# A Gram matrix from the high halves in 512-column matmuls, and image columns in the value product, in a two-layer cross-attention kernel

## The chip, the cores and the metric

The kernel runs on one core of a Trainium2 chip. The metric is the time of one execution on the device in microseconds (us), as a median of runs. The engines are TensorE (PE, matmuls; PEld is its weight load), VectorE (DVE), ScalarE (ACT), GpSimd (POOL), and SyncE (SP), which here issues nearly all of the DMA transfers, in the order of its queue.

## What is computed

Two cross-attention layers run one behind the other on the same text context, in fp32. Both have 16 batches of 256 queries, 20 heads of 16 columns, and a context of 256 tokens of 512 features. Layer 1 takes 77 of these as text and 179 as image tokens. In layer 2, which the change concerns, the last four are image tokens and the other 252 text. Layer 2, cut:

```python
probs_t = softmax(q @ k_t.T * scale)             # per head, over 252 text tokens
text_out = probs_t @ v_t
qsem = probs_t @ text_ehs                        # per head: 256 x 512
qsem = qsem / max(norm(qsem), EPS)               # _l2norm
ip_n = ip_ehs / max(norm(ip_ehs), EPS)
sem = qsem @ ip_n.T                              # per head: 256 x 4
probs_ip = softmax(q @ k_ip.T * scale + 0.5 * sem) * spatial_mask
out = (text_out + probs_ip @ v_ip) @ W_out + b_out + hidden_states
```

The kernel never forms qsem. With p a row of probs_t and E the text tokens, its product with an image token is p (E e_ip), four more columns beside the values, and its squared norm is the quadratic form p (E E^T) p^T. E E^T, 252 x 252 for each batch, is the Gram matrix.

## The kernel before

An fp32 operand is held as two halves, a rounded high one and a low one (the remainder), each in a form that PE reads fast. A product (`prod`, L325) is the sum high x high, high x low, low x high, over the tiles of 128 of the contraction: 12 matmuls for 512 features.

Layer 2 runs in 80 slots of one head group (4 heads) each, five slots to a batch (`slot1`); the slots of the layer before overlap with its beginning. In each slot, for two halves t of 128 rows, PE computes scores T of the slot (L1018) and scores S of a later slot with rows and columns exchanged (L1023), of which DVE takes the maxima (`mn`, L1024) and a copy of the image columns (`sr`, L1040). There is one bank pair for S, so the second S comes when both have been read. ACT takes the exponentials (L1030); PE multiplies them with the values (L1088, L1090). For the norm, PE multiplies the Gram blocks (`gm`, seven of 128 x 128: four high, three low) with the rounded exponentials `ctb`, seven matmuls of 512 columns for each t (L1075, in `norm1`); DVE multiplies and adds the results (L1078, L1080), with POOL's part (L1080) and POOL's low halves (L1066) beside it.

Around the slots run tasks of a batch, each a generator that yields between its steps: `keys1` (k1: three row blocks m of the keys, L651 or L325 on PE, the image columns on POOL, L652, the low half on DVE, L655, then out to memory, kd, and back in slot form, ks), `tokens1` (t1: values, Gram), the opening `o1` (queries: high and low halves `hq`, L706 to L709, product L725, out as qd and back as qs), the image softmax `i1` (u, L1159 and L1161) and the close `c1` (three row products of the image part, L1209 on PE, L1210 on DVE, the halves `ho` by ACT, L981, and DVE, L972 and L974, then the output product L725 and L996).

The table `STEPS` (L45) gives each step a slot time relative to its batch's first slot, in five fill positions (.2 apart) of each slot; a step is recorded when its time comes, so the order in which PE, DVE, ACT and POOL work in layer 2 is that of the program. `late` puts off a DVE evacuation to a fixed place behind the slot's own work. SP's queue is ordered by the scheduler.

`tokens1` has five steps: values of rows 0 to 127, values of rows 124 to 251 (DUP = 124; a mask `tmask` keeps double rows from counting twice), Gram of these two row blocks, and a last one that scales a block. A Gram step is one `prod`: the tokens are both operands, 12 matmuls of 256 columns. Columns 252 to 255 of the Gram product are E e_ip, which DVE multiplies with 1 / norm (`rn`) into the value tile (L679, L693); ACT rounds the others to `gm` (L675, L676, L683, L684) and DVE takes the low halves (L678, L687, L690).

## Time and profile before

| | |
|---|---|
| median of 3 runs | 1455.69 us (1451.59 to 1458.66) |
| profiled execution, span | 1449.8 us |
| PE busy in the span | 1401.7 us, 97% |
| DVE busy | 1174.2 us, 81% |
| POOL busy | 1152.3 us, 79% |
| ACT busy | 937.6 us, 65% |
| one batch of layer 2, steady | 48.15 us (five slots) |

The span is the profiled execution's own time; the runs have a few microseconds around it, 5.9 for the median. A row of a timeline gives the start, the time from the first start to the last end of the row's instructions, the engine, the line, the operation, out<-in by the program's names, partitions x elements, and the count; in brackets the idle time before, and what ended it. Matmuls overlap in the records, so what a run of them takes is read from start to start.

### The profile page before, as it was taken

How to read it: one execution, taken by the hardware profiler on the slowest of the kernel's cores; microseconds unless marked ns; L12 is line 12 of the kernel's file. 1: busy time of each engine (PE TensorE's matmuls, PEld its weight loads, DVE VectorE, ACT ScalarE, POOL GpSimd, SP SyncE). 2: the span in 40 equal slices, each digit the busy share in tenths (PEclk: the TensorE clock that was granted, in tenths of full speed). 3: DMA queues.
4: the chain of work that ended last, by engine and by line, in shares of the span. 5: the costliest groups of instructions: out<-in, count | busy, mean ns of one | idle time of the engine just before them, and what ended most of it. 6: DMA issues, size and time to landing. Idle time of an engine off the chain costs nothing.

```text
span 1449.8 us, 35042 instructions
## 1 busy us (share of the span) xinstructions
PE 1401.7 (97%) x12166; PEld 1157.8 (80%) x12166; DVE 1174.2 (81%) x2570; ACT 937.6 (65%) x2075; POOL 1152.3 (79%) x1181
## 2 busy tenths in 40 slices
PE   7899999999999999889999999999999999999998
PEld 6788888888888888577777788878878888888865
DVE  5477777777777788867888888988998889888887
ACT  5567676767676776755666666666666666566553
POOL 4269797979787878887778887788778877887785
PEclk9999999999999999999999999999999999999999
DMA  6866575665656578575544444544454445444411
GB/s 200 197 161 181 143 186 147 163 169 155 168 151 171 145 201 232 133 188 155 158 123 124 143 141 125 154 137 140 130 150 138 139 135 149 139 136 131 130 33 50
DMA packets 236284, 215.74 MB, mean 149 GB/s; under 512 B 57834, under 2 KB 222732, under 8 KB 236108
## 3 DMA queue, kind: packets, MB, share of 16 engines
q1 hardware_dynamic: 233886, 212.53, 53.4%
q8 instruction: 97, 1.59, 0.5%
q10 hardware_dynamic: 2222, 0.98, 0.3%
q14 instruction: 79, 0.65, 0.2%
HBM read 127.32 MB, written 85.16 MB: 147 GB/s over the span
## 4 chain that ended last, share of the span: by engine, by line
PE 52%; DVE 3%; POOL 1%; issue 1%; ACT 0%; DMA 0%; ACTq 0%; DVEq 0%; POOLq 0%
PE X L1075 18%; PE X L325 9%; PE X L725 6%; PE P L1088 5%; PE T L1018 4%; PE S L1023 3%; PE P L1090 2%; PE X L1209 1%; PE X L651 1%; PE P L1055 1%; DVE mn L1024 1%; PE P L934 1%; POOL P L902 0%; DVE wt L1078 0%; POOL wt L1066 0%
## 5 line engine op out<-in xcount | busy, mean ns | idle before, releaser
L902 POOL TENSOR_TENSOR P<-P,rs 128x512 f32<-128x512 f32 x320 | 412.4, 1313 | 136.1 <-ACT P L899 136.0
L1075 PE MATMUL X<-ctb,gm 128*128 128x512 f32 x1120 | 293.3, 403 | 0.7 <-DVE wt L1078 0.7
L1066 POOL TENSOR_TENSOR wt<-P,ctb 128x512 f32<-128x512 f32 x212 | 268.1, 1293 | 0.0
L899 ACT ACTIVATE P<-T 128x512 f32<-128x512 f32 x320 | 174.7, 594 | 101.8 <-PE T L896 83.7
L1024 DVE TENSOR_REDUCE mn<-S 128x4 fp32r<-128x1008 f32 x160 | 192.1, 1200 | 58.7 <-PE S L1023 56.8
L1075 PEld LDWEIGHTS X<-ctb,gm 128*128 128x128 f32 x1120 | 202.5, 190 | 38.5 <-DVE wt L1078 0.9
L1078 DVE TENSOR_TENSOR wt<-X,wt 128x512 f32<-128x512 f32 x240 | 159.7, 682 | 4.2 <-PE X L1075 3.9
L1030 ACT ACTIVATE P<-T 128x512 f32<-128x512 f32 x212 | 115.2, 598 | 58.3 <-PE T L1018 56.6
L1080 POOL TENSOR_TENSOR wt<-wt 128x512 f32<-128x512 f32 x80 | 103.5, 1294 | 60.2 <-DVE wt L1078 60.0
L876 DVE TENSOR_REDUCE mn<-S 128x4 fp32r<-128x716 f32 x160 | 142.5, 890 | 0.0
L1065 ACT ACTIVATE ctb<-P 128x512 fp32r<-128x512 f32 x212 | 122.4, 625 | 29.4 <-PE X L1075 20.6
L934 PE MATMUL P<-P,vr 128*32 128x256 f32 x1920 | 123.7, 388 | 0.0
L725 PE MATMUL X<-ho,wF 128*128 128x256 f32 x768 | 109.0, 286 | 2.2 <-DVE ho L974 1.2
L725 PEld LDWEIGHTS X<-ho,wF 128*128 128x128 f32 x768 | 100.5, 189 | 8.8 <-DVE ho L974 2.7
L725 PE MATMUL X<-hq,wE 128*128 128x256 f32 x720 | 102.7, 286 | 4.6 <-ACT hq L706 3.3
L725 PEld LDWEIGHTS X<-hq,wE 128*128 128x128 f32 x720 | 96.4, 193 | 8.3 <-ACT hq L706 3.8
L875 DVE TENSOR_REDUCE mn<-S 128x4 fp32r<-128x308 f32 x160 | 74.8, 468 | 23.2 <-PE S L874 22.9
L945 DVE STREAM_TRANSPOSE nt<-P 128x512 f32<-128x512 f32 x80 | 57.1, 714 | 39.2 <-PE P L934 38.9
L934 PEld LDWEIGHTS P<-P,vr 128*32 128x32 f32 x1920 | 56.1, 110 | 40.8 <-issue 4.9
L874 PE MATMUL S<-ks,qs 125*128 125x256 f32 x480 | 85.7, 301 | 2.2 <-DMA ks<-kd 1.7
L874 PEld LDWEIGHTS S<-ks,qs 125*128 125x128 f32 x480 | 64.4, 189 | 28.2 <-issue 24.1
L325 PE MATMUL X<-cta,wA 128*128 128x252 f32 (+3 forms) x534 | 78.8, 292 | 7.9 <-ACT wA L244 5.7
(231 smaller groups left out, 3275.3 us busy)
## 6 DMA issues: line engine op xcount, KB each, us to landing
qd<-q SPq DMA_DIRECT2D x80, 256.0 KB
qs<-qd SPq DMA_DIRECT2D x160, 112.0 KB
ks<-kd SPq DMA_DIRECT2D x160, 112.0 KB
rawc<-in_cT_dram SPq DMA_DIRECT2D x60, 256.0 KB
kd<-kst SPq DMA_DIRECT2D x50, 256.0 KB
qs<-qd SPq DMA_DIRECT2D x60, 192.0 KB
ks<-kd SPq DMA_DIRECT2D x60, 192.0 KB
qd<-q SPq DMA_DIRECT2D x64, 128.0 KB
```

What stands on the lines that cost most here:

```text
L325: last = mm(out, lhs(a, k), rhs(b, k), start=i == 0, stop=i == len(terms) - 1)
L725: mm(pp, w(s, k, slice(m * 128, (m + 1) * 128)), a[:, t], start=i == 0, stop=i == len(terms) - 1)
L874: mm(sp[:, h], Q[: XROW + T0, h, t * 128 : (t + 1) * 128], K[: XROW + T0, h], start=True, stop=True)
L876: anchor(nc.vector.tensor_reduce(mn[:, 1, :, t], sp[:, :, T0:], axis=AX.X, op=ALU.max))
L899: exp = anchor(nc.scalar.activation(pt, st[p], AF.Exp, scale=SCALE))
L902: anchor(nc.gpsimd.tensor_mul(pt, pt, rs[:, t : t + 1].to_broadcast([128, 2, S])))
L934: mm(pv[32 * s : 32 * s + 32, o : o + S], v[:, vt, h : h + 32], P[k, s // 2][:, t, s % 2], start=vt < 2, stop=vt != 1,)
L1024: anchor(nc.vector.tensor_reduce(maxes[k + 2][:, :, t], sp[:, :, :T1], axis=AX.X, op=ALU.max))
L1065: nc.scalar.activation(R[k, u][:, t], P[k, u][:, t], AF.Copy, scale=0.5)
L1066: anchor(nc.gpsimd.tensor_sub(W[k, u][:, t], P[k, u][:, t], f(R[k, u][:, t])))
L1075: mm(yp, gm[:, gb], R[k, u][:, kt], start=i == 0, stop=i == len(blocks[n]) - 1)
L1078: nc.vector.tensor_mul(product, yp, w[:, n])
```

## The change

**Gram.** A Gram step becomes four matmuls of 512 columns, one for each 128 features: the tokens' high half stands, and high and low halves of all 256 tokens move. The bank then holds g = high x high and x = high x low. The third term, low x high, is the transpose of x summed over both row blocks, and since the quadratic form is symmetric, the cross product may be doubled instead: the low blocks become g - rounded(g) + 2x. Where only one of two symmetric blocks is kept, the transposed cross block is needed: ACT copies it from the first Gram's bank (`turn`), and one 128-column matmul adds it, turned, in the second Gram's sum, behind its third 512-column matmul. DVE has two operations for each low block instead of one.

**Image columns.** They came from the Gram product with all three terms and now come from the value product, which grows from 320 to 324 columns. The value weights get four more columns at each side, into which POOL copies the batch's image tokens at step m = 1 of the keys (two copies). ACT copies the four columns out (`ip`), and DVE multiplies them with `rn` from there.

**Steps.** Times in the table move; in effect, in a steady batch: the third key block and its transfers, both value steps, both Gram steps, the last three steps of the opening, and steps of the image softmax and of the close. Line numbers grow by 2 to 26.

```diff
--- before.py
+++ after.py
@@ -54,18 +54,18 @@
     "s0o": (-2.4, -1.4, -1, -0.8, -0.4, 0.4, 1.6,),
     "c0e": (5.6, 6, 6.6, 7.2, 7.6, 8.2,),
     "c0o": (5.6, 6, 6.6, 7.2, 8.2, 9.2,),
-    "k1": (-7, -6.2, -6.2, -5, -4.2, -3.4,),
-    "t1": (-3.2, -2.2, -2.2, -1.4, -0.2,),
-    "o1": (-7, -6.8, -6, -5.8, -5.4, -3.4,),
-    "i1": (6.8, 7.6, 7.6, 8.8, 9.4, 9.6, 10.6, 10.8, 10.8, 12.2,),
-    "c1": (12.8, 12.8, 13.4, 14, 14, 15.8,),
-    ("i1", B - 2): (6.6, 7, 7.2, 7.2, 7.8, 8, 8.6, 9.2, 9.2, 9.6,),
+    "k1": (-7, -6.2, -6.2, -5, -4, -2.6,),
+    "t1": (-3.2, -2, -1.2, -1.2, -0.2,),
+    "o1": (-7, -6.8, -6, -4, -3.6, -0.6,),
+    "i1": (6.8, 8.2, 8.6, 8.6, 9, 9.6, 10.8, 10.8, 10.8, 12.2,),
+    "c1": (12.8, 12.8, 13, 13.6, 13.8, 17,),
+    ("i1", B - 2): (6.6, 7, 7.2, 7.2, 7.8, 8, 8.6, 8.8, 9.2, 9.6,),
     ("c1", B - 2): (9.8, 11.8, 11.8, 12.2, 12.4, 12.4,),
-    ("i1", B - 1): (6.8, 7.6, 7.8, 10, 10, 10, 11, 11, 11.2, 12,),
+    ("i1", B - 1): (6.8, 7.6, 7.8, 10, 10, 10, 11.2, 11.2, 11.2, 12,),
     ("c1", B - 1): (11.8, 11.8, 11.8, 11.8, 13.4, 16,),
-    ("k1", 0): (-7, -6.2, -5.8, -5, -4.6, -3,),
+    ("k1", 0): (-7, -6.2, -5.8, -5, -4.6, -3.4,),
     ("k1", 1): (-8, -6.2, -5.2, -5, -4.6, -3,),
-    ("t1", 0): (-3.6, -2.6, -2, -1.4, -0.4,),
+    ("t1", 0): (-3.6, -2.6, -1.2, -0.6, 0.4,),
     ("t1", 1): (-3, -2.2, -2.2, -1.2, -0.8,),
     ("o1", 0): (-7, -7, -5.6, -5.2, -4.4, -4.4,),
     ("o1", 1): (-6.8, -6.8, -6.2, -5.8, -4, -3.8,),
@@ -152,7 +152,7 @@
 
 
     clock = [-99.0]
-    words, slots = {"ctb": 1024, "cta": 1024, "raw": 512, "rawc": 512, "kb": 576, "mt": S, "mx": 2, "kst": 4 * S, "rs": 2 * S, "P": 4 * S}, {}
+    words, slots = {"ctb": 1024, "cta": 1024, "raw": 512, "rawc": 512, "kb": 576, "mt": S, "mx": 2, "kst": 4 * S, "rs": 2 * S, "P": 4 * S, "wC": 8 * (320 + 2 * NIP)}, {}
 
     def buf(tag, shape, dtype=F32, bufs=1, name=None):
         if tag in ("wB", "wD", "vr", "raw"):
@@ -217,6 +217,8 @@
     nc.scalar.copy(ident_r, ident)
     tmask = const_tile([128, 7], "tmask")
     dma(tmask, tmask_d)
+    tm2 = const_tile([128, 1], "tm2")
+    nc.vector.tensor_scalar_mul(tm2, tmask[:, 2:3], 2.0)
 
     anchors = {}
 
@@ -338,7 +340,13 @@
         yield from in_turn(parts, wait, *(("rawc raw", nc.vector) if b == 2 and n == 2 else ("rawc", nc.gpsimd)))
         if n == 2:
             return lambda s, k: tiles[k][:, s].rearrange("p (b t) -> p b t", b=2)
-        return lambda s, k: tiles[k // 2][:, s, (k % 2) * S : (k % 2 + 1) * S]
+
+        def view(s, k):
+            if isinstance(k, slice):
+                return tiles[k.start // 2][:, s].rearrange("p s (k t) -> p s k t", t=S)
+            return tiles[k // 2][:, s, (k % 2) * S : (k % 2 + 1) * S]
+
+        return view
 
 
     ct = [buf(t, [128, 2, 512], FR, bufs=2, name="ct") for t in ("cta", "cta", "ctb", "ctb")]
@@ -571,7 +579,9 @@
 
     def weights6():
         cip = w1["cip"]
-        _, text, w1["v"] = by_row(wv1_d, "wC")
+        wv = buf("wC", [128, 2, 4, 320 + 2 * NIP], FR)
+        text = [(wv1_d[k * 128 : (k + 1) * 128], wv[:, 0, k, NIP:-NIP], wv[:, 1, k, NIP:-NIP]) for k in range(4)]
+        w1["v"], w1["ip"] = lambda s, k, i: wv[:, s, k, NIP * i : NIP * i + 320 + NIP], lambda i: wv[..., (0, 320 + NIP)[i] :][..., :NIP]
         image, wvi1 = by_column(wvi1_d)
         yield from in_turn(text + image, 0.3, "rawc")
         vip = buf("rawc", [128, 512], bufs=2, name="vip")[:BI, :CP]
@@ -655,42 +665,58 @@
                 lambda kst=kst, kp=kp: nc.vector.tensor_sub(kst[:, 1, 0, :T1], kp, f(kst[:, 0, 0, :T1])),
                 lambda kst=kst, m=m: keys_out1(kd[1][b], m, kst[:, :, 0]),
             )
+            if m == 1:
+                for k in range(2):
+                    last = ct(slice(None), slice(2 * k, 2 * k + 2))[..., T1:]
+                    nc.gpsimd.tensor_copy(w1["ip"](b % 2)[:, :, 2 * k : 2 * k + 2], f(last))
             yield
 
     def tokens1(b):
         ct = ct1[b]
         V, G = v1t[b % 2], gmt[b % 2]
         vc = vcols(V, V1W)
-        for t, lo, sc in ((0, 0, 1.0), (1, DUP, tmask[:, 2:3])):
-            vp = bank()[:, :320]
-            prod(vp, lambda s, k: ct(s, k)[:, lo : lo + 128], w1["v"], 4)
-            nc.scalar.activation(vc[:, t, :, 0:16], vp.rearrange("p (h d) -> p h d", d=D), AF.Copy, scale=sc)
+        rnb = rn[:, 4 * b : 4 * b + 4].unsqueeze(1).to_broadcast([128, H, NIP])
+        tm = tmask[:, 2:3]
+        i = b % 2
+        for t, lo, sc in ((0, 0, 1.0), (1, DUP, tm)):
+            vp = bank()[:, : 320 + NIP]
+            prod(vp, lambda s, k: ct(s, k)[:, lo : lo + 128], lambda s, k: w1["v"](s, k, i), 4)
+            own = vp[:, NIP * (1 - i) :][:, :320].rearrange("p (h d) -> p h d", d=D)
+            nc.scalar.activation(vc[:, t, :, 0:16], own, AF.Copy, scale=sc)
+            ip = buf("ip", [128, NIP], bufs=2)
+            nc.scalar.activation(ip, vp[:, 320 * i :][:, :NIP], AF.Copy, scale=sc)
+            ipb = ip.unsqueeze(1).to_broadcast([128, H, NIP])
+            late(lambda t=t, ipb=ipb: nc.vector.tensor_mul(vc[:, t, :, 17:21], ipb, rnb))
             yield
-        rnb = rn[:, 4 * b : 4 * b + 4].unsqueeze(1).to_broadcast([128, H, NIP])
+        turn = buf("turn", [128, 128], FR)
         for t, lo in ((0, 0), (1, DUP)):
-            g = bank()[:, :S]
-            prod(g, lambda s, k: ct(s, k)[:, lo : lo + 128], ct, 4)
-            ip = g[:, T1:S].unsqueeze(1).to_broadcast([128, H, NIP])
+            bk = bank()
+            for k in range(4):
+                both = ct(slice(None), k)
+                mm(bk.rearrange("p (s t) -> p s t", s=2), ct(0, k)[:, lo : lo + 128], both, start=k == 0, stop=k == 3)
+                if t and k == 2:
+                    mm(bk[:, S : S + 128], turn, ident_r, start=False, stop=False)
+            g, x = bk[:, :S], bk[:, S:]
             if t == 0:
                 nc.scalar.copy(G[:, 0, :], g[:, 0:128])
                 nc.scalar.copy(G[:, 1, 4:], g[:, 128:T1])
-                late(
-                    lambda g=g: nc.vector.tensor_sub(G[:, 4, :], g[:, 0:128], f(G[:, 0, :])),
-                    lambda ip=ip: nc.vector.tensor_mul(vc[:, 0, :, 17:21], ip, rnb),
-                )
+                nc.scalar.copy(turn, x[:, DUP:T1])
+
+                def first_lows(g=g, x=x):
+                    nc.vector.tensor_sub(G[:, 4, :], g[:, :128], f(G[:, 0, :]))
+                    nc.vector.scalar_tensor_tensor(
+                        G[:, 4, :], x[:, :128], 2.0, f(G[:, 4, :]), op0=ALU.mult, op1=ALU.add
+                    )
+
+                late(first_lows)
             else:
-                tm = tmask[:, 2:3]
                 nc.scalar.activation(G[:, 2, :], g[:, 0:128], AF.Copy, scale=tm)
                 nc.scalar.activation(G[:, 3, 4:], g[:, 128:T1], AF.Copy, scale=tm)
 
-                def corrected(g=g, ip=ip):
-                    nc.vector.scalar_tensor_tensor(
-                        G[:, 5, :], g[:, 0:128], tm, f(G[:, 2, :]), op0=ALU.mult, op1=ALU.subtract
-                    )
-                    nc.vector.scalar_tensor_tensor(
-                        G[:, 6, 4:], g[:, 128:T1], tm, f(G[:, 3, 4:]), op0=ALU.mult, op1=ALU.subtract
-                    )
-                    nc.vector.scalar_tensor_tensor(vc[:, 1, :, 17:21], ip, tm, rnb, op0=ALU.mult, op1=ALU.mult)
+                def corrected(g=g, x=x):
+                    for to, high, at, own in ((G[:, 5, :], G[:, 2, :], slice(0, 128), tm), (G[:, 6, 4:], G[:, 3, 4:], slice(128, T1), tm2)):
+                        nc.vector.scalar_tensor_tensor(to, g[:, at], tm, f(high), op0=ALU.mult, op1=ALU.subtract)
+                        nc.vector.scalar_tensor_tensor(to, x[:, at], own, f(to), op0=ALU.mult, op1=ALU.add)
 
                 late(corrected)
             yield
```

The rows below show how the instructions stand in a steady batch. First DVE, from the last correction (L1080, now L1106) of the slot that has two row products of the close to the first maxima of the next slot (L1024, now L1050). Before:

```order
L1080 TENSOR_TENSOR wt<-wt,X 128x512
L1210 TENSOR_TENSOR X<-hT_10095,X 128x256 x2
L972 TENSOR_TENSOR ho_239<-X,ho_239 128x256 x2
L678 TENSOR_TENSOR gm<-X,gm 128x128
L679 TENSOR_TENSOR v1t<-X,rn 128x20x4
L1024 TENSOR_REDUCE mn_558<-S 128x4
L1040 COPY sr_9041<-S 128x2x2x4
L1024 TENSOR_REDUCE mn_558<-S 128x4
```

Now:

```order
L1106 TENSOR_TENSOR wt<-wt,X 128x512
L1236 TENSOR_TENSOR X<-hT_10088,X 128x256 x2
L998 TENSOR_TENSOR ho_241<-X,ho_241 128x256 x2
L1236 TENSOR_TENSOR X<-hT_10088,X 128x256
L1000 SCALAR_TENSOR_TENSOR ho_241<-ho_241,tmask,X 128x256
L1050 TENSOR_REDUCE mn_560<-S 128x4
L1066 COPY sr_9034<-S 128x2x2x4
L689 TENSOR_TENSOR v1t<-ip_8915,rn 128x20x4
L1050 TENSOR_REDUCE mn_560<-S 128x4
L1066 COPY sr_9034<-S 128x2x2x4
L1104 TENSOR_TENSOR wt<-X,wt 128x512
L1187 SCALAR_TENSOR_TENSOR u_10104<-u_10104,tmp_855 128x40
```

The third row product and its half of ho (L1236, L1000) have moved ahead of the maxima, the first Gram's low half has left, and u (L1187), which stood in the slot before, follows the second maxima.

Second, PE in the same two slots (`cta` are the context tokens, `wC` the value weights). Before, from the norm's products to the next slot's T:

```order
L1075 MATMUL X<-ctb_84,gm 128x512 x7
L1075 MATMUL X<-ctb_85,gm 128x512 x7
L1209 MATMUL X<-rs_508,rs_507 128x256 x2
L325 MATMUL X<-wC_157,cta_82 128x320 x6
L325 MATMUL X<-wC_157,cta_83 128x320 x6
L325 MATMUL X<-cta_82 128x256 x6
L325 MATMUL X<-cta_83 128x256 x6
L1018 MATMUL T<-qs_190,ks_194 128x256 x4
```

Now, from the norm's products of the slot behind it to its end:

```order
L1101 MATMUL X<-ctb_87,gm 128x512 x4
L751 MATMUL X<-ho_241,wF_1009 128x256 x8
L1101 MATMUL X<-ctb_87,gm 128x512 x3
L751 MATMUL X<-ho_241,wF_1009 128x256 x8
L696 MATMUL X<-cta_84 128x512 x2
L696 MATMUL X<-cta_85 128x512 x2
L696 MATMUL X<-cta_84 128x512 x2
L696 MATMUL X<-cta_85 128x512
L698 MATMUL X<-ident_r,turn_9102 128x128
L696 MATMUL X<-cta_85 128x512
L751 MATMUL X<-hq_297,wE_89 128x256 x8
L1044 MATMUL T<-qs_191,ks_195 128x256 x4
```

Both Gram products (L696) and the turn (L698) now stand together at the end of the later slot, between the output product and the query product.

Third, POOL around the third key block (L652, now L662) and the low halves for the norm (L1066, now L1092). Before:

```order
L1080 TENSOR_TENSOR wt<-wt 128x512
L1066 TENSOR_TENSOR wt<-P_97,ctb_84 128x512 x2
L652 CAST kst_237<-kip 128x2x4
L1066 TENSOR_TENSOR wt<-P_98,ctb_85 128x512 x2
L1159 TENSOR_TENSOR u_10135<-tmp_852 128x40
```

Now:

```order
L1106 TENSOR_TENSOR wt<-wt 128x512
L1092 TENSOR_TENSOR wt<-P_99,ctb_86 128x512 x2
L1092 TENSOR_TENSOR wt<-P_100,ctb_87 128x512 x2
L1185 TENSOR_TENSOR u_10104<-tmp_854 128x40
L662 CAST kst_239<-kip 128x2x4
```

The image part of the third key block has moved behind the second pair of low halves and behind u's operation.

## The prediction

> **What bounds the kernel now.** The page comes first: how busy each engine is, and which engine holds the chain of work that ended last.
>
> ```profile
> span 1449.8 us, 35042 instructions
> ...
> PE 1401.7 (97%) x12166; PEld 1157.8 (80%) x12166; DVE 1174.2 (81%) x2570; ACT 937.6 (65%) x2075; POOL 1152.3 (79%) x1181
> ...
> PE 52%; DVE 3%; POOL 1%; issue 1%; ACT 0%; DMA 0%; ACTq 0%; DVEq 0%; POOLq 0%
> ```
>
> TensorE carries the chain, but a mean over the span hides its stages. The windows of busy time by stage (PE, weight load, DVE, ACT, POOL, then the granted clock) separate layer 1's tail from a steady batch of layer 2:
>
> ```profile
> 600.00:650.00 50.00, 42.37 (x405) 34.34 (x405) 39.74 (x82) 30.10 (x62) 44.02 (x45) 1.00 0.65 165
> 989.20:1037.40 48.20, 48.20 (x409) 39.05 (x409) 43.03 (x90) 30.12 (x67) 39.48 (x43) 1.00 0.49 142
> ```
>
> In layer 2 PE never idles at full clock, and DVE has 5.2 us left of 48.2. The steps of batches 0 and 1 run beside layer 1, where PE is idle 7.6 us of 50, so PE work saved there is worth little. I count 14 batches. The timeline of PE shows the two of a batch's five slots that the change touches, which I call the second (from 1019.96) and the third (from 1030.25), and where the next begins:
>
> ```profile
> 1019.96 0.50 PE L1018 MATMUL T<-qs,ks 57*128 57x256 f32 x4
> ...
> 1022.80 3.48 PE L1075 MATMUL X<-ctb,gm 128*128 128x512 f32 x14
> 1026.11 1.02 PE L1209 MATMUL X<-rs,rs 128*128 128x256 f32 x4
> 1026.79 2.10 PE L325 MATMUL X<-wC,cta 128*128 128x320 f32 x12
> 1028.72 1.59 PE L325 MATMUL X<-cta 128*128 128x256 f32 x12
> 1030.25 0.51 PE L1018 MATMUL T<-qs,ks 57*128 57x256 f32 x4
> 1030.59 0.41 PE L1023 MATMUL S<-ks,qs 56*128 56x256 f32 x4
> ...
> 1032.69 0.48 PE L1023 MATMUL S<-ks,qs 56*128 56x256 f32 x4
> ...
> 1036.19 1.59 PE L325 MATMUL X<-cta 128*128 128x256 f32 x12
> 1037.62 0.86 PE L1075 MATMUL X<-ctb,gm 128*128 128x512 f32 x3
> ...
> 1040.46 1.12 PE L725 MATMUL X<-hq,wE 128*128 128x256 f32 x8
> 1041.51 0.50 PE L1018 MATMUL T<-qs,ks 57*128 57x256 f32 x4
> ...
> 1068.12 0.50 PE L1018 MATMUL T<-qs,ks 57*128 57x256 f32 x4
> ```
>
> Read the distances between starts, since pipelined ends overlap. The second and third slots take 1041.51 - 1019.96 = 21.55 us, the other three 26.61.
>
> **The PE term.** Removed: both Gram products, 1.53 (1028.72 to 1030.25) and 1.43 (1036.19 to 1037.62), 2.96 us. Added: eight 512-column matmuls at 3.31 / 14 = 0.236, the pitch of L1075 (1022.80 to 1026.11), 1.89; the turning matmul of 128 columns, half of a 256-column one (1.43 / 12 = 0.12), 0.06; four columns on each of 24 value matmuls, 96 columns at 0.236 / 512, 0.04. PE alone gains 0.97 us a batch, times 14 = 13.6.
>
> [...]
>
> **Does DVE let PE take it?** Order, not load, decides. The timeline of DVE through the same two slots:
>
> ```profile
> 1022.85 1.21 DVE L1024 TENSOR_REDUCE mn<-S 128x4 fp32r<-128x1008 f32 x1 [0.71 <-PE S L1023]
> ...
> 1026.78 0.93 DVE L1161 SCALAR_TENSOR_TENSOR u<-u,tmp 128x40 f32<-128x40 f32 x1
> 1027.62 0.69 DVE L1078 TENSOR_TENSOR X<-X,wt 128x512 f32<-128x512 f32 x1
> ...
> 1028.95 0.75 DVE L1210 TENSOR_TENSOR X<-hT,X 128x256 f32<-128x256 f32 x2
> 1029.81 0.75 DVE L972 TENSOR_TENSOR ho<-X,ho 128x256 fp32r<-128x256 f32 x2
> ...
> 1031.25 1.20 DVE L1024 TENSOR_REDUCE mn<-S 128x4 fp32r<-128x1008 f32 x1
> ...
> 1033.21 1.21 DVE L1024 TENSOR_REDUCE mn<-S 128x4 fp32r<-128x1008 f32 x1 [0.68 <-PE S L1023]
> ...
> 1035.94 1.26 DVE L709 SCALAR_TENSOR_TENSOR hq<-hq,tmask,xq 128x256 fp32r<-128x256 f32 x1
> 1037.12 0.68 DVE L1078 TENSOR_TENSOR wt<-X,wt 128x512 f32<-128x512 f32 x1
> 1037.72 0.41 DVE L1210 TENSOR_TENSOR X<-hT,X 128x256 f32<-128x256 f32 x1
> ...
> 1038.65 0.46 DVE L974 SCALAR_TENSOR_TENSOR ho<-ho,tmask,X 128x256 fp32r<-128x256 f32 x1
> ...
> 1039.62 0.30 DVE L693 SCALAR_TENSOR_TENSOR v1t<-X,tmask,rn 128x80 f32<-128x80 f32 x1
> 1039.83 0.69 DVE L1078 TENSOR_TENSOR X<-X,wt 128x512 f32<-128x512 f32 x1
> ...
> 1043.50 0.87 DVE L996 SCALAR_TENSOR_TENSOR xc<-X,bo,xc 128x256 f32<-128x256 f32 x2
> ```
>
> After the change the third row product of the close (L1210, L974) stands in the second slot, ahead of the third slot's first reduction of S. One pair of row products costs PE 0.34 (1026.11 to 1026.79 for two pairs), so PE's second slot shrinks from 10.29 to 10.29 - 1.53 + 0.34 + 0.02 = 9.12 us. DVE's doesn't shrink with it. From the second slot's start: the reduction at +2.89; to the third correction +3.93 (4.77, less the 0.84 of u, L1161, which now stands in the third slot): 6.82; +1.33 to the row products (1027.62 to 1028.95): 8.15; +0.86 to L972: 9.01; two of these 0.69 (0.75 less 0.06 of overlap): 9.70; the third row product and its trip over ACT to L974, 0.93 (1037.72 to 1038.65), less 0.08 because no correction of DVE's stands between any more, 0.85; L974 itself 0.45: 11.0. The first reduction starts at +11.0, was +11.29.
>
> PE has one S buffer and writes the second S once the first is reduced and copied, 1.44 after that reduction (1031.25 to 1032.69): at +12.44. By its own work it would be there at 9.12 + 2.44 = 11.56. **A wait of 0.9 us on DVE takes nearly the whole gain.** Behind that S stand 11.46 - 2.44 = 9.02 us of PE work (both slots by PE alone, 21.55 - 0.97 = 20.58; the third 20.58 - 9.12 = 11.46), which ends the pair at 21.46.
>
> Two things then lie on the same stretch. The turn: ACT copies the first Gram's two halves and then the cross block before PE may turn it. Three copies of the size of L693's operation on DVE (0.21 from start to start, 1039.62 to 1039.83, at least) take 0.6, and 0.2 to start and to hand over; three 512-column matmuls, 0.71, stand between on PE, and the turn's weights load after. I put 0.25 on PE; the bounds are nothing (the copies start as the bank's halves fill) and the whole 0.8. At 0.25 the pair ends at 21.71, at 0.8 at 22.26, 0.7 over the old 21.55 and 10 us in all. The other is DVE up to the token product L725 on hq, whose bank the slot's last correction frees (L1080 before). The page-wide group of hq's low half (busy us, mean ns, then the idle time before it) prices the one operation there that was disturbed:
>
> ```profile
> L709 DVE SCALAR_TENSOR_TENSOR hq<-hq,tmask,xq 128x256 fp32r<-128x256 f32 x32 | 28.1, 878 | 1.5 <-ACT hq L706 1.5
> ```
>
> The second reduction starts 0.52 behind the second S (1032.69 to 1033.21), at 12.96; +2.73 to hq (1033.21 to 1035.94), 15.69; u, 0.84, 16.53; hq 0.80 (its mean of 0.88 less overlap) to 1.18 (here, 1035.94 to 1037.12), 17.33 to 17.71; two corrections at 0.60 (1037.12 to 1037.72), 18.53 to 18.91; xc 0.40 (half of 0.87, less overlap), 18.93 to 19.31; the last two 1.33 (1027.62 to 1028.95) and 0.15 until PE has the bank, 20.41 to 20.79; the product's own 1.05 (1040.46 to 1041.51): 21.46 to 21.84. PE's way and DVE's both end near 21.65, **+0.10 us a batch**. DVE's bounds are -0.09 and +0.29; times 14, -1.3 to +4.1. I take the middle, +1.4, because PE's way lies there too.
>
> **What I cost at nothing.** DVE's three further operations a batch (5 become 8, about 0.21 each, as L693) go into its 5.2 us; were they all ahead of PE, they would cost 0.63 x 14 = 9. ACT's three (two image copies, the turn) go into 18 us of idle; POOL's two tiny copies into 8.7. The second Gram needs a bank that xc's evacuation frees; its DVE place is inside the sum above.
>
> **The sum.** 1449.8 + 1.4 = 1451.2 profiled, and the runs' median stands 5.9 above the profiled span (1455.69 - 1449.8): **1457 us**.
>
> **Rivals.**
>
> PE stays the bound, chance 0.30: the waits of DVE in the rows above (0.71 and 0.68 us ahead of a reduction) are slack that it gives up first, and its operations run nearer each other than the starts that I added. Then 13.6 to 11 us come off: 1442 to 1445. For it: no PE idle in the windows. Against: DVE would have to gain 0.9 us between the two reductions.
>
> Late keys, slower, chance 0.20. Keys of the third 128 rows (L652) come on POOL behind a second pair of L1066 now:
>
> ```profile
> 1021.17 0.21 POOL L652 CAST kst<-kip 128x8 fp32r<-128x8 f32 x1
> 1021.32 2.54 POOL L1066 TENSOR_TENSOR wt<-ksl,ctb 128x512 f32<-128x512 f32 x2
> 1023.81 0.27 POOL L1159 TENSOR_TENSOR u<-tmp 128x40 f32<-128x40 f32 x1
> ```
>
> ```profile
> 1021.41 2.54 SPq L139 DMA_DIRECT2D kd<-kst  x4
> ...
> 1025.45 2.52 SPq L139 DMA_DIRECT2D ks<-kd  x6
> ```
>
> SP writes the keys out (kd, 2.54) and reads them back 1.5 behind (1023.95 to 1025.45); the second of these reads has been issued at 1026.29 (a third of 2.52 on), and the third slot's S wants it at 1030.59, a cover of 4.3 us. POOL's step now comes 2.8 later (2.54 + 0.27), and SP has one more transfer ahead (0.4, as one issue below). PE wants the keys 0.5 later: thirteen of L725's matmuls more stand in the slot before (13 x 1.05 / 8 = 1.7), the second slot is 1.17 shorter. So 1.6 of the cover is left before PE idles, and 2.5 before the time moves, since PE waits 0.9 for DVE anyway. From issue to use such a read takes 1.5 at least, as kd does here; layer 1's first bounds it above:
>
> ```profile
> 40.46 0.41 SPq L139 DMA_DIRECT2D ks<-kd  x1
> ...
> 44.16 0.71 PE L874 MATMUL S<-ks,qs 125*128 125x256 f32 x4 [1.67 <-DMA ks<-kd]
> ```
>
> 44.16 - 40.87 = 3.3. So it decides from 2.5 on, and at 3.3 costs 0.8 a batch: 1457 + 11 = 1468. For it: the order on POOL. Against: 3.3 is seen once, in layer 1 alone, and the 1.5 of this stage is far under 2.5. [...] No run here shows the landing in this stage.
>
> Other slower ways, 0.04: the whole turn on PE, 1449.8 + 10 + 5.9 = 1466, or the three DVE operations ahead of it. The remaining 0.46 is the forecast. That the change isn't done as it says is excluded: the 512-column instructions stand in its program.
>
> **The numbers.** A change under 0.5%, 1448.4 to 1463.0, is about what a measurement of this kernel can't tell from none. Forecast 0.46 (1451 to 1462 by itself: the bounds -1.3 and +4.1, and the spread of the runs), faster 0.30, slower 0.24. The range takes in the PE rival and the late keys: 1441 to 1468.
>
> **What would show it.** Right: in the third slot the second S starts behind sr's copy with PE idle near 0.9 us; second slot 9.1 us, third 12.5; PE below 48 of 48.2, period 48.1 to 48.4. PE rival: period 47.2, S without idle. Late keys: PE's T or S in the third slot waiting for DMA of ks. A wait ahead of the turn above 0.7 or ahead of the second Gram on DVE would refute what I cost at little. I would be wrong above all if DVE's reduction comes well before +11.0.

## The result, and the profile after

The changed kernel took **1502.53 us** (median of 4 runs, 1498.75 to 1506.12) against 1456.11 for the kernel before beside it: a ratio of 1.0333 (95% interval 1.0300 to 1.0365). It is slower by 3%, and the forecast of 1457 us with its range up to 1468 missed. The page after: the span, busy times, and the chain that ended last.

```profile
span 1497.0 us, 34757 instructions
...
PE 1412.0 (94%) x11926; PEld 1145.3 (77%) x11926; DVE 1210.0 (81%) x2619; ACT 943.8 (63%) x2123; POOL 1152.2 (77%) x1213
...
PE 72%; DMA 12%; DVE 6%; POOL 4%; issue 3%; SPq 2%; ACT 2%; ACTq 0%; DVEq 0%; POOLq 0%
```

Transfers (DMA) hold 12% of the chain; before, the page had 0%. The window of a typical batch (same columns as before) shows PE idle 3.3 us, where it had idled 0:

```profile
1198.81:1250.25 51.44, 48.16 (x393) 37.83 (x393) 45.03 (x93) 30.59 (x70) 39.48 (x46) 1.00 0.47 131
```

51.44 - 48.15 = 3.29 us a batch, times 14 = 46, nearly the whole loss (1497.0 - 1449.8 = 47). Not all of the loss is waiting: between 800 and 1400 us a batch takes 51.3 us in the mean, so twelve of them lose 38; PE's listed waits there make 30.3, and four stretches of 3.41 us at a granted clock of 0.50 (last section) another 7 by estimate (four times half of 3.41). PE's timeline of its second slot (from 1198.81) and third slot (from 1208.17) shows where:

```profile
1198.81 0.51 PE L1044 MATMUL T<-qs,ks 57*128 57x256 f32 x4
...
1208.17 0.50 PE L1044 MATMUL T<-qs,ks 57*128 57x256 f32 x4
1209.75 1.00 PE L1049 MATMUL S<-ks,qs 56*128 56x256 f32 x4 [1.07 <-DVE X L1236]
...
1212.45 0.41 PE L1049 MATMUL S<-ks,qs 56*128 56x256 f32 x4
...
1218.05 1.09 PE L696 MATMUL X<-cta 128*128 128x512 f32 x4
1221.18 0.95 PE L696 MATMUL X<-cta 128*128 128x512 f32 x3 [2.04 <-DVE xc L1022]
...
1223.65 0.51 PE L1044 MATMUL T<-qs,ks 57*128 57x256 f32 x4
```

The second slot takes 9.36 us and the third 15.48, 24.84 together against 21.55; the other three are unchanged at 26.60. PE stands 1.07 us at the first S and 2.04 us ahead of the second Gram, whose bank the output's evacuation xc (L1022) frees. Over 600 us (850 to 1450):

```profile
PE X L696 <- DVE xc L1022: 18.5, 10, 2.7
PE S L1049 <- DVE X L1236: 5.2, 6, 1.2
PE S L1049 <- DMA ks<-kd: 3.4, 7, 1.1
```

(us in all, times, longest.) The profile puts the wait of S in the batch above down to DVE, but it is one for late keys: S came at 1209.75, while DVE's L1236 had ended at 1209.01 and touches nothing that S reads or writes. SP was issuing key reads up to 1211.1, with the reload of xc among them (below), and the chain has a key read from 1207.22 to 1210.20, with the other three matmuls of S right behind it (1210.25). That the other waits of S put down to L1236 are late keys too is read from this one. Why is DVE late with xc? The rows of SP, ACT and DVE in the same batch:

```profile
1205.40 0.54 SPq L139 DMA_DIRECT2D out_dram<-xc  x1
...
1208.43 0.38 SPq L139 DMA_DIRECT2D xc<-x1d  x1
1208.86 2.23 SPq L139 DMA_DIRECT2D ks<-kd  x5
...
1212.77 0.38 SPq L139 DMA_DIRECT2D sid<-sr  x1
```

```profile
1213.62 0.24 ACT L1083 CAST mt<-P 8x128 fp32r<-8x128 f32 x1
1216.47 0.53 ACTq L1085 DMA_DIRECT2D qs<-mt  x1
1217.04 0.83 ACT L732 CAST hq<-xq 128x768 fp32r<-128x768 f32 x1 [3.19 <-DMA sid<-sr]
```

```profile
1208.59 0.42 DVE L1236 TENSOR_TENSOR X<-hT,X 128x256 f32<-128x256 f32 x1
...
1217.91 1.63 DVE L735 SCALAR_TENSOR_TENSOR hq<-hq,tmask,xq 128x256 fp32r<-128x256 f32 x1 [2.04 <-ACT hq L732]
...
1220.65 0.47 DVE L1022 SCALAR_TENSOR_TENSOR xc<-X,bo,xc 128x256 f32<-128x256 f32 x1
```

ACT has the maxima `mt` at 1213.9, but its transfer qs<-mt goes only at 1216.47, and the profile puts the 3.19 us that ACT stands idle down to sid<-sr (the copied scores on their way to memory). The two share no data; why ACT's transfer comes only behind sid<-sr is in no view. On ACT the cast of hq (1217.04) stands behind this transfer, DVE's half of hq (1217.91) behind that, then two corrections (1219.46), then xc (1220.65). The chain of waits of another batch gives the links back to the start (start, us, piece):

```profile
1050.85 3.92 DMA out_dram<-xc
...
1054.79 3.69 DMA xc<-x1d
...
1058.55 4.57 DMA sid<-sr
...
1063.19 1.62 DMA qs<-mt
...
1067.47 0.40 DVE xc L1022
```

The close's last step had moved from 15.8 to 17, into the second slot. Its store of xc, the reload of the same buffer (which waits for the store), the scores out and the maxima stand in one row, each waiting for the one ahead.

### The profile page after: what moved, and what is told of

The parts are those of the page before. It is cut to its first block, busy times and chain, and to the rows that moved or that the text cites. A ratio compares the mean times of both kernels' runs of the same rounds, so it can differ in the third digit from the quotient of the medians.

```text
span 1497.0 us, 34757 instructions
## 1 busy us (share of the span) xinstructions
PE 1412.0 (94%) x11926; PEld 1145.3 (77%) x11926; DVE 1210.0 (81%) x2619; ACT 943.8 (63%) x2123; POOL 1152.2 (77%) x1213
## 3 DMA queue, kind: packets, MB, share of 16 engines
q8 instruction: 96, 1.57, 0.5%
## 4 chain that ended last, share of the span: by engine, by line
PE 72%; DMA 12%; DVE 6%; POOL 4%; issue 3%; SPq 2%; ACT 2%; ACTq 0%; DVEq 0%; POOLq 0%
PE X L327 16%; PE X L1101 12%; PE X L751 10%; PE P L960 7%; PE S L900 6%; PE T L922 5%; PE P L1114 4%; PE T L1044 3%; PE S L1049 2%; DMA xc<-x1d 2%; PE P L1116 2%; DMA sid<-sr 2%; DMA ks<-kd 2%; POOL wt L1092 2%; SPq L139 2%
## 5 line engine op out<-in xcount | busy, mean ns | idle before, releaser
L1101 PE MATMUL X<-ctb,gm 128*128 128x512 f32 x1120 | 282.5, 399 | 0.0
L1092 POOL TENSOR_TENSOR wt<-P,ctb 128x512 f32<-128x512 f32 x212 | 267.7, 1292 | 0.3 <-ACT ctb L1091 0.3
L1050 DVE TENSOR_REDUCE mn<-S 128x4 fp32r<-128x1008 f32 x160 | 192.7, 1204 | 56.0 <-PE S L1049 53.3
L1106 POOL TENSOR_TENSOR wt<-wt 128x512 f32<-128x512 f32 x80 | 103.1, 1288 | 42.8 <-DVE wt L1104 42.1
L733 POOL TENSOR_TENSOR hq<-xq,hq 128x512 fp32r<-128x512 f32 x29 | 37.9, 1306 | 80.6 <-ACT hq L732 80.6
L1049 PE MATMUL S<-ks,qs 56*128 56x256 f32 x640 | 73.6, 294 | 20.6 <-DVE X L1236 6.0
```

Source lines behind the costliest of these rows:

```text
L1050: anchor(nc.vector.tensor_reduce(maxes[k + 2][:, :, t], sp[:, :, :T1], axis=AX.X, op=ALU.max))
L1092: anchor(nc.gpsimd.tensor_sub(W[k, u][:, t], P[k, u][:, t], f(R[k, u][:, t])))
L1101: mm(yp, gm[:, gb], R[k, u][:, kt], start=i == 0, stop=i == len(blocks[n]) - 1)
```

## The experiments

Ratios are to the kernel before on the same chip, with 95% intervals. Waits are PE's between 800 and 1400 us of the profiled run (us in all, times, longest). Where a kernel takes image columns from PSUM, lines after L689 count one more.

**Code or steps?** Each half of the change alone.

```diff
# code_oldsteps: after, with all changed rows of STEPS as before
-    "c1": (12.8, 12.8, 13, 13.6, 13.8, 17,),
+    "c1": (12.8, 12.8, 13.4, 14, 14, 15.8,),
...
# old_newsteps: before, with the changed rows of STEPS
```

> The changed code with the whole step table of before. Transfers theory (the moved steps bring late transfers, the code itself saves PE work): PE's 0.97 us a batch comes through at least in part, 1442 to 1456 us, and the first row block's Gram waits for no bank. Code theory (the 512-column Gram, its turn and its two further DVE operations are what is slow, at any steps): 1475 us or more. Note that this kernel differs from the changed one in the table alone.

> The code of before with the whole step table of the change. Transfers theory: as slow as the changed kernel or slower, since PE also keeps its 0.97 us a batch: 1495 to 1520 us, with the scores' maxima transfer on ACT (qs<-mt) waiting for sid as there. Code theory: within 10 us of before, 1446 to 1466.

The code alone: 1.0231 (1.0216 to 1.0246). The steps alone: 1.0324 (1.0309 to 1.0340). Both together cost no more than the steps (1.0333), so the two losses do not add; by their waits, below, both lie mainly in the third slot. The transfers' theory holds for the steps (ACT's cast of hq waits for sid there too, 31.8 us in 11 times, 4.1 at most), but not for the whole, since the code loses without them. Waits of the code alone, then of the steps alone:

```profile
PE X L751 <- DVE wt L1106: 15.8, 12, 1.3
PE S L1049 <- DVE sr L1066: 6.6, 11, 0.6
```

```profile
PE X L325 <- DVE xc L996: 14.3, 9, 2.5
PE S L1023 <- DMA ks<-kd: 6.7, 10, 2.0
```

**The transfers' chain.** One link undone at a time: the close's last step; a second buffer for xc, so that the reload waits for no store; and ACT's issue of the third slot's qs<-mt, put behind the cast of hq.

```diff
# c1last
-    "c1": (12.8, 12.8, 13, 13.6, 13.8, 17,),
+    "c1": (12.8, 12.8, 13, 13.6, 13.8, 15.8,),
# xc2
-        x = buf(tag, [128, 3, S])
+        x = buf(tag, [128, 3, S], bufs=2 if tag == "xc" else 1)
# mt_later
-        late(lambda: nc.scalar.dma_start(f(row), f(mt)))
+        (later if k % 5 == 4 else late)(*([0.3] if k % 5 == 4 else []), lambda: nc.scalar.dma_start(f(row), f(mt)))
```

> The changed kernel with one number put back: the close's last step (output product, store of xc) at 15.8 in place of 17. Transfers theory: store and reload of xc leave the second slot's part of SP's queue, sid goes out some 2 us earlier, ACT's qs<-mt no longer waits for it, and the 2.2 us a batch that PE waits for DVE's xc ahead of the second Gram go: 14 x 2.2 = 30 off, 1462 to 1475 us, the late keys (1.2 us a batch) stay. Order theory (the third row product ahead of the reduction of S on DVE, the bank of the second Gram): unchanged, 1495 us or more.

> The changed kernel with two buffers for xc, so that the reload waits for no store; the order on PE, ACT, DVE and POOL is unchanged, SP's is not (store and reload now stand behind sid). Transfers theory: sid goes out about 2 us earlier, the keys' reads come without a stop, and qs<-mt on ACT waits for the first si (about 3 us behind sid, 2 to land) in place of sid: 0.9 to 2.2 us a batch off, 1472 to 1490 us. Order theory: unchanged, 1495 us or more.

> The changed kernel, where ACT issues the transfer of the maxima (qs<-mt) of the third slot behind the rounding of hq and the first pair of ctb, not ahead of them; all else as it is. Transfer theory (ACT stands still at that transfer because it has to wait for sid, the eighth transfer before it, so hq, DVE's corrections, xc and with them the bank of the second Gram come late): hq is rounded right behind mt's copy, some 2.5 us earlier in the slot, PE's wait ahead of the second Gram (2 us) goes, 14 x 2 = 28 off: 1470 to 1480 us. Rival (DVE by itself is late: operations with both operands in SBUF wait for POOL): the wait ahead of the second Gram shifts by less than 0.5, 1490 to 1502 us.

c1last 1.0191 (1.0174 to 1.0208): 20 us came back, two thirds of the 30 expected, and its 1479 us lie outside the range. xc2 1.0328 (1.0309 to 1.0348): a miss. mt_later 1.0244 (1.0215 to 1.0274): 13 us came back, half of the 28 expected, and its 1490 us miss that range too. Their waits follow in that order: for c1last the wait that the edit was to remove (18.5 us in the changed kernel; the largest that c1last has left is S behind the copy sr, 9.0 us), for xc2 its largest and the row of ACT that tells why, for mt_later its two largest:

```profile
PE X L696 <- DVE xc L1022: 4.2, 6, 2.0
```

```profile
PE X L696 <- DVE xc L1022: 23.6, 11, 2.8
...
1107.92 0.83 ACT L732 CAST hq<-xq 128x768 fp32r<-128x768 f32 x1 [3.97 <-DMA si<-sid]
```

```profile
PE X L698 <- ACT turn L703: 10.9, 10, 1.9
PE S L1049 <- DMA ks<-kd: 7.0, 10, 2.5
```

With two buffers S waited less for keys (1.7 us for DMA, 4.7 in the changed kernel), but ACT's cast of hq behind qs<-mt now stood 3.97 us for si<-sid (in the changed kernel's batch 3.19 for sid<-sr). That sid is the eighth transfer ahead of qs<-mt, as mt_later's expectation has it, was my count in the program; that this count decides is not shown. With the issue put off, the wait ahead of the second Gram was gone, and PE stood at the turn instead: ACT, idle up to 4.0 us at a time ahead of `r` (L1191), the first of its operations behind the transfer's new place, copied the cross block late.

**Two operands in SBUF.** DVE's image-column operation reads `ip`, an SBUF copy, where it had read PSUM. Here ACT's copies are left out and DVE reads the bank (for the second row block its operation takes the mask along), with old steps, and then with the new ones and the close's step undone. The copies and the place of the operand change together and are not told apart.

```diff
# old_ip (on code_oldsteps), c1_ip (on c1last)
-            ip = buf("ip", [128, NIP], bufs=2)
-            nc.scalar.activation(ip, vp[:, 320 * i :][:, :NIP], AF.Copy, scale=sc)
-            ipb = ip.unsqueeze(1).to_broadcast([128, H, NIP])
+            ipb = vp[:, 320 * i :][:, :NIP].unsqueeze(1).to_broadcast([128, H, NIP])
# c1_ip_k1: c1_ip, and
-    "k1": (-7, -6.2, -6.2, -5, -4, -2.6,),
+    "k1": (-7, -6.2, -6.2, -5, -4.2, -3.4,),
# c1_ip_k1_mt: c1_ip_k1, and mt_later's edit
```

> The changed code at the step table of before, with DVE reading the image columns from the PSUM bank of the value product (as it read them from Gram's bank before), without ACT's copies. Port theory (the new operation has both operands in SBUF and stands behind POOL's instruction, 0.74 and 0.47 us in place of 0.23, with 0.16 for ACT's copy): the third slot's first reduction starts 0.6 to 0.8 us earlier, 14 x 0.7 = 10 off the 1485 us of this code at these steps: 1472 to 1478. Rival (the doubled cross product: three more operations a batch for the Gram's low blocks on DVE): 1482 to 1488, unchanged.

> The changed kernel with the close's last step at 15.8 and the image columns read from PSUM by DVE. Port theory: the 1.36 us operation ahead of the second slot's first reduction becomes 0.25, PE's wait of 0.7 us for the second S there goes: 10 off 1479: 1466 to 1471 us. Rival (the late keys decide in the slot behind it anyway): 1476 to 1482.

old_ip 1.0167 (1.0150 to 1.0184), 9 us less than the same with the copies, where 7 to 13 were expected. c1_ip 1.0217 (1.0198 to 1.0236), a miss: no faster than c1last. S still waited 13.6 us in all, 4.3 of them put down to the reads of the keys, and eight stretches ran at half clock (the granted clock was 0.98 in the mean from 800 to 1100 us and from 1100 to 1400, and 0.50 from 1202.00 to 1203.50); that the rest were late keys as well is not shown. The operation's own times (ns min/median/max, all of layer 2's steady part), with the SBUF copy in the changed kernel and from PSUM in old_ip:

```profile
L689 DVE TENSOR_TENSOR v1t<-ip,rn x23: 233/590/1411, 800.3 to 1365.0; 128x80 f32<-128x80 f32 x23
```

```profile
L688 DVE TENSOR_TENSOR v1t<-X,rn x12: 208/210/217, 835.9 to 1388.8; 128x80 f32<-128x80 f32 x12
```

The second line is the first row block's operation; the second block's, with the mask, takes 0.30 to 0.31 us. At old_ip's steps, but with the SBUF copy (code_oldsteps), the operation takes the 0.74 and 0.47 us that old_ip's expectation names.

**Keys and ACT's queue.** c1_ip with the third key block's steps undone, and then with ACT's issue put off as well.

> The run before it with the close's last step at its old time and the image columns from PSUM (1485.8) had late keys of the third 128 rows in its steady part (13.6 us of S waiting) and eight half-clock windows. This one also takes the third key block's steps back to their old times (-4.2, -3.4). Late-keys theory: S's waits for keys go, and the half-clock windows with them, since only those waits left PE idle that long; 13.6 us and some 8 times 1.8 us can come back, part of it into S waiting for sr: 1460 to 1472, and no window below 0.9 in layer 2's steady part. Rival: the wait is SP's queue and not POOL's order, the keys are late all the same: 1480 to 1488.

> The changed kernel with four things undone (the close's last step at 15.8, the third key block at its old times, image columns from PSUM, and the third slot's maxima transfer qs<-mt issued behind the cast of hq). Without the last it stood at 1480.9, with 3.2 us a batch of ACT waiting for sid and 1.9 of PE ahead of the second Gram. Queue theory: the wait ahead of the second Gram goes, 1.9 times 14 = 27 at most, less 0.6 to 0.8 a batch ahead of the turn, which both Grams in one slot leave: 1462 to 1470. Rival: the wait only moves to the turn, as it did where this was tried with the other three left in: 1474 to 1482.

c1_ip_k1 1.0191 (1.0174 to 1.0208), a miss: S's waits for keys fell to 1.7 us, but the time hardly moved, because the wait ahead of the second Gram took their place; and the granted clock, 1.00 in the mean from 800 to 1100 us, was 0.98 from 1100 to 1400. Its 1481 us lie in the rival's range, though not for the rival's reason. c1_ip_k1_mt **1.0059** (1.0039 to 1.0080), as the queue theory had it. Waits of the first, then of the second:

```profile
PE X L697 <- DVE xc L1023: 21.0, 12, 3.0
PE S L1050 <- DMA ks<-kd: 1.7, 2, 1.0
```

```profile
PE X L699 <- ACT turn L704: 7.0, 9, 2.0
PE S L1050 <- DVE sr L1067: 3.6, 9, 0.9
```

So with the new steps, undoing the close's step, the third key block's, ACT's early issue and the image columns' copies together gives back some four fifths of the loss (1.0333 to 1.0059). The image columns' part in it was not tried by itself; against c1last, c1_ip shows no gain from it. Undone one by one, each hands its time to the next.

**Which half of the code?** Image columns in the value product alone, read from PSUM, with before's Gram and steps.

> The image half of the code alone: image columns in the value product, read by DVE from PSUM, before's Gram of two halves and three terms, before's steps. It splits the code's loss (1479.1 with the new Gram as well). If the loss lies in the new Gram and what ACT and DVE do for it: 324 instead of 320 columns cost 0.02 a value step and nothing waits: 1453 to 1459, PE waits in the steady part under 2 us in all, as before. Rival: the value product's bank, held by two readers now, delays the third slot: 1465 to 1475.

1.0008 (0.9992 to 1.0024): no change. The new Gram costs the 1.6% that old_ip has.

**The Gram in another place.** On old_ip: Gram steps as the changed kernel has them and hq's low half on DVE one correction later (v4h); then u behind the maxima (v5a); the second Gram in the slot after (v5d); both there (v5f). The expectations of v5a and v5d call the Gram steps that they start from spread; in v4h and v5a they stand together, both at -1.2.

```diff
# v4h
-    "t1": (-3.2, -2.2, -2.2, -1.4, -0.2,),
+    "t1": (-3.2, -2, -1.2, -1.2, -0.2,),
-            after_next(third)
+            soon.append([3, third])
# v5a, v5d, v5f: v4h, and
-    "i1": (6.8, 7.6, 7.6, 8.8, 9.4, 9.6, 10.6, 10.8, 10.8, 12.2,),
+    "i1": (6.8, 8.2, 8.2, 8.8, 9.4, 9.6, 10.6, 10.8, 10.8, 12.2,),
# t1 in v5d (-3.2, -2, -1.2, -0.8, -0.2), in v5f (-3.2, -2, -0.8, -0.4, -0.2)
```

> The changed code with the table of before except tokens' steps (both Gram products at the end of the third slot, as in the change), image columns from PSUM, and DVE's low half of hq one correction later, so that it doesn't stand beside POOL's hq. Transfer and port theories together: no late transfer, the first Gram's low blocks out of the third slot's reductions, hq 0.75 in place of 1.26: PE is the bound again but for 0 to 0.4 us a batch, 1438 to 1446 us, against 1451 before. Rival (the 512-column Gram or its turn costs PE by itself): 1465 us or more.

> The kernel at 1472.5 (new code, Gram steps spread again, image columns from PSUM, hq's low half one correction later) with the image softmax's second and third step at 8.2 instead of 7.6, so that u (0.93 us) stands behind the third slot's reductions of S instead of ahead. DVE-order theory: the 0.35 us a batch that S waits for sr goes: 1466 to 1469, and the wait of 0.6 ahead of the turn stays. Rival: u only pushes hq back, and hq's product waits instead: 1472 to 1476.

> As v5a, and the second Gram one position later, in the slot after, behind hq's product (steps -2, -1.2, -0.8 instead of the spread ones). The turn's copies on ACT are then long done and hq's product gets a bank that DVE frees early. Theory that the remaining loss is waits for ACT's turn (0.6 a batch), sr (0.35) and banks (0.3 and 0.25): about 1.3 us of 1.5 a batch go, times 14 = 18: 1450 to 1458, with PE waits in the steady part under 0.4 us a batch. Rival: the banks are full whatever stands where, and a wait for a bank of DVE's comes back in the next slot: 1465 to 1475.

> As v5d, with both Grams in the slot after hq's product (-0.8, -0.4), so that the third slot loses 0.95 us of PE and the next gains it. Theory that the third slot is bound by DVE's chain (reductions, hq, corrections, xc): PE's work taken out of it is not missed there and costs 0.95 in the next slot, unless that is bound by DVE as well: 1455 to 1466. Rival: the pair is bound by PE once the banks are free, then it equals v5d within 3 us.

v4h 1.0132 (1.0110 to 1.0155), v5a 1.0245 (1.0221 to 1.0270), v5d 1.0245 (1.0229 to 1.0261), v5f 1.0425 (1.0406 to 1.0444). All missed: each place has its own wait. The largest in v4h is the turn, as both Grams stand together; in v5a the turn again, worse, since ACT's copy stands behind ho's cast, which stands behind a slower hq on DVE (1.58 us, 0.47 in v4h); in v5d it is ho on DVE (12.1 us), with 14.0 put down to the casts of the tokens cta; in v5f ho on DVE:

```profile
PE X L699 <- ACT turn L704: 8.8, 13, 0.8
```

```profile
PE X L699 <- ACT turn L704: 23.4, 12, 2.0
```

```profile
PE X L752 <- DVE ho L1001: 22.4, 12, 1.9
```

(v4h, v5a and v5f.)

**DVE's order in the third slot.** On old_ip, with the Gram steps spread as before: the first Gram's two DVE operations put off from ahead of the maxima to behind ho's low half (v8a), with hq's half one correction later too (v7d), by 0.7 slots instead of 0.8 (w70), and with u moved (w70u).

```diff
# v8a
-                late(first_lows)
+                (later(0.8, first_lows) if clock[0] >= NS else late(first_lows))
# v7d: v8a, and
-            after_next(third)
+            soon.append([3, third])
# w70: v7d with later(0.7, first_lows); w70u: w70 with v5a's row "i1"
```

> New code, before's steps, image columns from PSUM (1479.1, with 1.3 us a batch of hq's product waiting for the slot's last correction on DVE and 0.3 of S waiting for sr), and the first Gram's two operations on DVE for the low half put off until behind ho's low half, ahead of the second Gram's four. They leave their place ahead of the third slot's first reduction (0.5 us), and their bank, not the last correction's, becomes hq's. Theory that the rest of the code's loss is this order and this bank: both waits go, 1.3 and 0.3 times 14 = 22: 1455 to 1461, the hq wait under 0.3 a batch. Rival: DVE ahead of the second half's products is the bound wherever the two operations stand, and PE waits ahead of another bank: 1470 to 1479.

> As the run before it, and hq's low half on DVE one correction later, so that PE's last norm product of the slot finds its bank 0.7 us sooner and hq's product its operand 0.6 later. If PE would wait for that bank (0.3 to 0.4 a batch): 1450 to 1457, under the run before it. Rival: hq's product is reached by DVE too late then, equal or up to 8 us over it.

> The kernel at 1464.5 (new code, before's steps, image columns from PSUM, the first Gram's two operations put off, hq's half one correction later) ran eight batches at 48.4 and the last four at 51.2 us, where the two operations had slipped behind the last correction by rounding of the slot time, and hq's product then waited 1.9. Here they are put off by 0.7 slots instead of 0.8, so that all batches have the order of the eight. Order theory: the four lose 2.8 each, 11 us: 1451 to 1455. Rival: something else slows the last batches: over 1460.

> As the run before it, and u (0.94 us beside POOL) behind the third slot's maxima instead of in the second slot, so that ho's halves leave DVE 0.9 us sooner and the third slot's S finds its bank. Order theory: the first S's 0.2 and the second's 0.2 a batch go: 1446 to 1451, under before. Rival: hq's half comes to run beside POOL's part of hq, as with u moved before (1.58 instead of 0.47), and hq's product waits: 1455 to 1475.

v8a 1.0133 (1.0100 to 1.0166), v7d 1.0074 (1.0054 to 1.0095), w70 **1.0023** (1.0012 to 1.0034), 1456.43 us, w70u 1.0084 (1.0064 to 1.0104). v8a fell short of its range: PE's last norm product waited for its bank (6.3 us in 12 times), and the slip that w70 mends cost it too. v7d was nearly as wide off, until w70 showed why: with the order the same in all batches they take 48.4 us each, and the time falls by 8 us (from 1464.5), where 11 were expected, to 3.4 above before (1453.02) and 1.4 above its range. w70u missed, as its rival had it: moving u let the third slot's S follow T without a wait, but made DVE's half of hq start together with POOL's part of it, and PE then waited 9.9 us in all for ho, which stands behind hq on DVE. The rows in w70u (DVE, POOL), and then in w70:

```profile
1043.13 1.57 DVE L736 SCALAR_TENSOR_TENSOR hq<-hq,tmask,xq 128x256 fp32r<-128x256 f32 x1
```

```profile
1043.12 1.30 POOL L734 TENSOR_TENSOR hq<-xq,hq 128x512 fp32r<-128x512 f32 x1 [3.51 <-ACT hq L733]
```

```profile
1040.96 0.72 DVE L736 SCALAR_TENSOR_TENSOR hq<-hq,tmask,xq 128x256 fp32r<-128x256 f32 x1
```

```profile
1040.10 1.31 POOL L734 TENSOR_TENSOR hq<-xq,hq 128x512 fp32r<-128x512 f32 x1 [2.89 <-ACT hq L733]
```

DVE's operation ends 0.28 and 0.27 us behind POOL's in both, whenever it started. No version was found that beats the kernel before. What w70 still pays shows in PE's timeline at its third slot's end:

```profile
1033.34 1.08 PE L697 MATMUL X<-cta 128*128 128x512 f32 x4
1034.35 0.50 PE L1045 MATMUL T<-qs,ks 57*128 57x256 f32 x4
...
1045.41 0.38 PE L1045 MATMUL T<-qs,ks 57*128 57x256 f32 x1
1046.20 0.39 PE L1045 MATMUL T<-qs,ks 57*128 57x256 f32 x2 [0.40 <-DVE wt L1107]
...
1055.36 0.50 PE L1045 MATMUL T<-qs,ks 57*128 57x256 f32 x4
```

The third slot takes 11.06 us, 0.20 less than before (11.26), but in the next, T waits for the third slot's last correction on DVE (L1107). That slot takes 9.95, and in the kernel before 9.15 (from the T at 993.32 to the T at 1002.47):

```profile
993.32 0.50 PE L1018 MATMUL T<-qs,ks 57*128 57x256 f32 x4
...
1002.47 0.51 PE L1018 MATMUL T<-qs,ks 57*128 57x256 f32 x4
```

What the Gram saves PE in two slots, DVE's longer chain takes back in the slot behind them.

## Why the prediction was wrong

**The PE term held.** In w70 the first Gram goes from 1.53 to 1.01 us (1033.34 to 1034.35) and the second, with the turn, from 1.43 to 1.02 (1040.62 to 1041.64): 0.93 off, forecast 1.01 for these parts. The products got cheaper by nearly what was said; the time did not. The second slot as a whole took 9.36 us in the changed kernel, where 9.12 were priced.

**DVE's place of the first reduction held.** The steps as priced put it at +11.0. The last operation ahead of it (L1000, 1209.45 and 0.48) ended at +11.1 in the changed kernel. But DVE had no S to reduce, since PE's first S was late for want of keys, and the reduction began at +11.98 (1210.79). The wait of 0.9 us ahead of the second S, on which the forecast rests, did not come: PE went from its late first S to the second (1212.45) without idling.

**The step that failed: the transfers of the moved close.** I followed the moved steps through PE, DVE, ACT and POOL, and from the close's last step I took only xc's 0.40 on DVE. Its store, the reload of the buffer and what is queued behind them (the scores out, qs<-mt on ACT) had no term, and the sentence that the second Gram's bank "is inside the sum" assumed that hq starts on time. ACT stood 3.19 us ahead of its cast in the batch shown, and PE 2.04 ahead of the bank. c1last (20 us back) and c1_ip_k1_mt (from 1.0191 to 1.0059 by ACT's issue alone) show it. The sign against itself that the prediction named, a wait ahead of the second Gram on DVE, came.

**Costed at nothing, wrongly: DVE's further operations.** I took 0.21 us each and DVE's 5.2 idle us as cover. In the changed kernel's trace they take 0.28 to 0.35 (gm, as the low halves in the kernel before, 0.29 to 0.35) and 0.59 in the median (image columns), and with the old steps they stand in the slot that sets the end, ahead of banks that PE needs (15.8 us of waits for hq's product in code_oldsteps). Idle time in other slots covers none of it. The code alone, without a moved step, lost 33 us: 9 by the image columns' copies and their operand in SBUF (old_ip), and of the 24 that stay, 21 by the order of DVE's operations (w70, 1.0167 to 1.0023), with the bank that hq's product gets changing along with it. The two were moved by the same edits and are not told apart.

**hq's low half was mis-sized.** I priced 0.80 to 1.18; it took 1.63, as it started with POOL's part. Its length differs with where POOL's part stands, from 0.47 us in v4h to the 1.63 here (last section), so a mean over 32 of them is no price for one place.

**The turn.** Bounds of nothing to 0.8 us held in the changed kernel, where the bank wait covered it; with that gone it rose to 1.1 a batch (mt_later, 10.9 in 10). The 0.2 us for start and hand-over in this term, and the 0.15 until PE has a bank in DVE's, stood without a row, and no run shows them. In the changed kernel the second Gram starts 0.06 us behind the end of xc (1221.12 to 1221.18). The lower bound, copies that start as the bank's halves fill, is in no row either: ACT's first copy of the second Gram starts at 1222.52, 0.04 behind the end of the Gram's last matmul (1222.03 and 0.45).

**The rivals.** PE as the bound fell: no kernel with the new Gram ran faster than the kernel before. No run shows the 11 us that I put at the lower end of its gain; the two Gram products' 0.93 in w70, times 14, make 13. Late keys were there, 1.07 us at the S of the batch shown, but the 1468 that I gave them was reckoned alone. The key read in the chain of that batch took 2.98 us from issue to landing (1207.22 to 1210.20), between the bounds of 1.5 and 3.3 and over the 2.5 from which keys decide. Undoing the key block's steps takes the wait for keys away (c1_ip_k1), so that the moved block makes them late was right; that the cover of 2.5 us went to the reload of xc, which stands among the key reads on SP, is read from its rows and was not tried by itself. The loss as it came, several queues in one slot, was none of the cases.

## What to carry to other kernels

A product that gets cheaper gains only where its engine ends last, and here every bank that it needs comes free on another engine's schedule: price the chain of evacuations in that slot first. When a step moves, follow its transfers as far as its arithmetic, up to the buffer that they reload and whichever engine issues the transfer that waits for them. Undoing one part may gain little because the next wait stands right behind; undo them in a growing set.
